# Making three of four one-hot matrices on ScalarE, and other distances in the perceptrons of a graph network

## The chip, the cores and the metric

The kernel runs on one core of a Trainium2 chip. A core has five engines that work side by side and wait for each other through semaphores: TensorE (PE in the profile; its weight loads are PEld), VectorE (DVE), ScalarE (ACT), GpSimd (POOL) and SyncE (SP). The metric is the device time of one execution in microseconds, as the median of three runs. Beside the runs there is one profiled execution, whose trace tells when each instruction ran and what it waited for.

## The reference

The input is 16 graphs (batches) of 1024 nodes with 64 features, and an adjacency of 16 x 1024 x 1024. Four layers follow each other, each with a residual and a layer norm. The first two are matrix products with the adjacency (with a perceptron in the first, with a division by the row sums in the second). The last two are what most of the kernel's time goes into:

```python
nd = adj_d > 0                       # the thinned-out neighbours, and the node itself
vals = jnp.where(nd[..., None], x[:, None, :, :], jnp.inf)
s = jnp.sort(vals, axis=2)           # per node and feature, over the neighbours
...                                  # quantiles 0.25, 0.5, 0.75, interpolated,
...                                  # summed with weights 0.25, 0.5, 0.25 into agg
out = (1.0 + EPS_GIN) * x + agg
h = jax.nn.relu(out @ W1 + b1)
y = h @ W2 + b2
```

So each node sorts its neighbours' features, 64 columns apart from each other, takes three quantiles, and passes the result through a perceptron of two matrix products. Which neighbours count is found once for a graph and serves both layers.

## The kernel before, in words

The nodes of a graph are put in order of the number of their neighbours and cut into eight tiles of 128 nodes. A tile t has room for `SIZES[t]` neighbours: 10, 11, 13, 14, 15, 17, 19 and 33. For each tile the features of the neighbours stand in slots, and a sorting network of minima and maxima runs over the slots on DVE.

The work goes in 18 rounds (`sort_round`). Round k sorts for two members: batch k in the first quantile layer and batch k - 2 in the second. So rounds 2 to 15 have two members, rounds 0, 1, 16 and 17 one. Within a round the seven shorter tiles come first and the long tile, of 33 slots, last.

The slots of the shorter tiles are filled by gathers: POOL issues an indirect DMA for each slot (`gather`, line 362), 92 for a member, from a table in DRAM. A ring of 60 slots (`ROOM`) lets the gathers run some tiles ahead. The slots of the long tile are filled without a gather, by `fill(k)`: for slot i a one-hot matrix `hot` says which node stands in slot i of each row (it is 1 where `e.place` equals i), and `pick` (line 358) multiplies it on PE with the features, split into three bf16 parts, 24 matmuls for each slot. Each group of four slots is copied from PSUM by ACT (line 742, `empty`), and two PSUM areas (`pgs`) take turns. There are six buffers for one-hot matrices (`HOTS`). A matrix is made on DVE by one comparison, or on ACT by two activations: `far` is the distance |place - i| (line 750), and Relu(1 - far) is the matrix (line 752). Before the change ACT makes the matrix of every fourth slot (i % 4 == 3), asked for two slots ahead, and DVE the others, each just ahead of its picks.

After a sort, `weigh` multiplies the wanted slots with the quantile weights on ACT (line 781) and adds them on DVE; `finish` is the perceptron with its layer norm (`settle`). In `finish` the two halves of the nodes go through two matmuls (lines 809 and 816), with an activation between, and a DVE addition `y = pd + b2r` ends each half. Its result for the first quantile layer, x3, is scattered by POOL into a table (line 826), from which the gathers of two rounds later read; `read_back` loads it for the picks of the long tile. For the second layer the same scatter writes the output.

The order of instructions on DVE, ACT and PE is fixed when the program is built, by a planner (`Weave`). All work other than the sorting is a set of Python generators. A `yield n` says that the next piece is due n us of DVE time later, where the DVE time is the sum of the estimated durations of the DVE instructions issued so far (`Metered`; its helper's line 207 stands for nearly all of DVE's instructions in the profile). After each instruction of the sort, `catch_up` issues all pieces that are due. `weave.add(gen, lag, pace)` enters a generator; the pace multiplies all of its distances. `weave.finish` forces a generator to its end, jumping over the distances left. Each engine takes its instructions in the order in which they were issued.

Other generators in the weave: `features` (the first two layers of the next batches), `lists` and `ordered` (the thinned neighbours, the order of nodes, the lists for the gathers). They use ACT for signs with a running sum (lines 526, 570, 585), distances (541) and copies of codes (618), whose results DVE takes up.

Of the kernel before, what the change touches and what calls it, by code (L numbers as in the profile page):

```python
# [13 lines left out]
F16 = mybir.dt.float16  # L14
BF = mybir.dt.bfloat16
I32 = mybir.dt.int32
U8 = mybir.dt.uint8
AF = mybir.ActivationFunctionType
ALU = mybir.AluOpType
AX = mybir.AxisListType  # L20

P = 128
# [7 lines left out]
HOTS = 6  # L30
# [68 lines left out]
def cut_pair(t, view, shift=0):  # L99

    s, m, stride, o, length = view
    s += shift
    if m == 1:
        return t[:, :, s + o : s + o + length, :]
    return t[:, :, s : s + m * stride, :].rearrange("p e (m s) w -> p e m s w", m=m)[:, :, :, o : o + length, :]
# [107 lines left out]
def adj_resnorm_kernel(ctx: ExitStack, tc: tile.TileContext, x, adj_t, nodemask, w01, b01, w02, b02,  # L213
                       w21, b21, w22, b22, w31, b31, w32, b32, out):
    nc = tc.nc
    B, N, C = x.shape
    NT = N // P
# [3 lines left out]
    s = SimpleNamespace()  # L221
    dve = Metered(nc.vector)
# [30 lines left out]
    minus_k = const.tile([P, KW], F32, name="minus_k")  # L253
    nc.gpsimd.iota(minus_k, pattern=[[-1, KW]], base=0, channel_multiplier=0, allow_small_or_imprecise_dtypes=True)
    one_f = const.tile([P, 1], F32, name="one_f")
# [50 lines left out]
    for t, want in enumerate(wants):  # L306
        for first, m, stride, length in regular_runs(want):
            for r in range(m):
                k = first + r * stride
# [44 lines left out]
    def pick(dst, hot, parts, first=True):  # L354

        for c in range(NT):
            for q in range(3):
                nc.tensor.matmul(dst, hot[:, c, :], parts[:, c, q, :], start=first and c + q == 0,  # L358
                                 stop=c == NT - 1 and q == 2)
# [364 lines left out]
    def members(k):  # L724

        return [(m, b, entries[b]) for m, b in enumerate((k, k - 2)) if 0 <= b < B]

    def fill(k):

        while k and (k - 1, NT - 1) not in free:  # L730
            yield 1
        t = NT - 1
        size = SIZES[t]
        got = tails[k] = s.lists.tile([P, 2, size, C], F32, name="got", tag="got_l", bufs=1)
        for m, b, e in members(k):
            while e.parts[m] is None or e.xs[m] is None or e.place is None or e.none is None:
                yield 1
            nc.scalar.copy(got[:, m, 0, :], e.xs[m][:, t, :])
            waiting = None

            def empty():
                nc.scalar.copy(got[:, m, waiting[0] : waiting[0] + 4, :], waiting[1])  # L742

            for i in range(1, size):
                if i % 4 == 1:
                    first, pg = i, pgs[i // 4 % 2]
                if i % 4 == 1:

                    far = s.work.tile([P, NT, P], F16, name="far", bufs=1)
                    nc.scalar.activation(far, e.place, AF.Abs, bias=minus_k[:, i + 2 : i + 3])  # L750
                    by_act = s.lists.tile([P, NT, P], BF, name="hot", bufs=HOTS)
                    nc.scalar.activation(by_act, far, AF.Relu, bias=one_f, scale=-1.0)  # L752
                if i % 4 == 3:
                    hot = by_act
                else:
                    hot = s.lists.tile([P, NT, P], BF, name="hot", bufs=HOTS)
                    dve.tensor_scalar(hot, e.place, float(i), None, op0=ALU.is_equal)
                whole = i < LEAST[t]
                if not whole:
                    nc.tensor.matmul(pg[:, i - first, :], e.none,  # L760
                                     ident_b[: KW - 1, i - 1 : i].to_broadcast([KW - 1, C]), start=True, stop=False)
                pick(pg[:, i - first, :], hot, e.parts[m], whole)
                yield 2.4
                if i % 4 == 2 and waiting:
                    empty()
                if i % 4 == 0:
                    waiting = first, pg
            yield 5
            empty()
            yield 0.5  # L770
            e.filled[m] = True
# [21 lines left out]
    def finish(b, e, layer, agg):  # L793

        xc = e.xs[layer]
        w1s, b1c, w2s, b2r = mlps[layer]
        y = s.work.tile([P, NT, C], F32, name="y_m", bufs=1)
        dve.tensor_add(agg, agg, xc)
        yield 2
        for h in range(NH):  # L800
            pt = s.psum.tile([P, HALF], F32, name="pt", tag="m", bufs=1)
            for q in range(G):
                nc.tensor.transpose(pt[:C, q * P : (q + 1) * P], agg[:, h * G + q, :], ident)
            yield 7
            o_t = s.work.tile([C, HALF], F32, name="o_t", bufs=1)
            nc.scalar.copy(o_t, pt[:C])
            yield 3
            ph = s.psum.tile([P, HALF], F32, name="ph", tag="m", bufs=1)
            nc.tensor.matmul(ph[:H], w1s, o_t, start=True, stop=True)  # L809
            yield 7  # L810
            h_t = s.work.tile([H, HALF], F32, name="h_t", tag="o_t", bufs=1)
            nc.scalar.activation(h_t, ph[:H], AF.Relu, bias=b1c)
            yield 3
            pd = s.psum.tile([P, G, C], F32, name="pd", tag="m", bufs=1)
            for q in range(G):
                nc.tensor.matmul(pd[:, q, :], h_t[:, q * P : (q + 1) * P], w2s, start=True, stop=True)  # L816
            yield 9
            dve.tensor_add(y[:, h * G : (h + 1) * G], pd, b2r[:, None, :].to_broadcast([P, G, C]))
        dve.tensor_mul(y, y, e.mask[:, :, None].to_broadcast([P, NT, C]))
        dve.tensor_add(y, y, xc)  # L820
        xn = agg if layer else s.feat.tile([P, NT, C], F32, name="x3s", bufs=3)
        yield from settle(xn, y, "m")
        yield 1
        dst, rows = (out_rows_of, e.out_rows) if layer else (table[1][b % 3], e.rows)
        for t in range(NT):
            put = nc.gpsimd.indirect_dma_start(  # L826
                out=dst, out_offset=bass.IndirectOffsetOnAxis(ap=rows[:, t : t + 1], axis=0), in_=xn[:, t, :],
                in_offset=None)
            tc.declare_no_dep(put.ins, group=f"rows{layer}{b}", reason="they write different rows")
            tc.add_to_no_dep_group(f"rows{layer}{b}", put.ins)  # L830
        if layer == 0:
            e.xs[1] = xn
            weave.add(read_back(b, e, dst))

    def read_back(b, e, src):

        while b and not entries[b - 1].filled[1]:
            yield 2
        x3 = s.feat.tile([P, NT, C], F32, name="x3", bufs=1)
        nc.sync.dma_start(x3, src[:N, :].rearrange("(t p) c -> p t c", p=P))  # L840
        yield 60
        parts = s.feat.tile([P, NT, 3, C], BF, name="x3p", bufs=1)
        yield from split(x3, parts, x3)
        e.parts[1] = parts
# [42 lines left out]
    weave = Weave()  # L887
# [42 lines left out]
    def finish_round(k, agg, sums):  # L930
        for gen in sums:
            while weave.runs(gen):
                yield 1
        for m, b, e in members(k):
            yield from finish(b, e, m, agg[:, m])

    def sort_round(k):

        if k >= 2:
            weave.finish(rounds[k - 2])  # L940
        filling = weave.add(fill(k), 4.0, 0.7 if k < 3 else 1.0)
        first = members(k)[0][0]
        which = slice(first, first + len(members(k)))
        agg = s.feat.tile([P, 2, NT, C], F32, name="agg")
        sums = []
        for t in (*reversed(range(NT - 1)), NT - 1):
            if t == NT - 1:
                weave.finish(filling)
                got = tails[k]
            else:  # L950
                n = order_of_tiles.index((k, t))
                fetch(n)
                got = gots[n]
            other = s.lists.tile([P, 2, SIZES[t], C], F32, name="other", bufs=1)
            pair = got[:, which], other[:, which]
            for is_max, d, v, i, j, to in usual[t]:
                dve.tensor_tensor(cut_pair(pair[to], v, d if is_max else 0), cut_pair(pair[i], v),
                                  cut_pair(pair[j], v, d), op=ALU.max if is_max else ALU.min)
                weave.catch_up()
                fetch()  # L960
            if len(sums) >= 2:
                weave.finish(sums[-2])
            sums.append(weave.add(weigh(k, t, got, agg, which)))
            weave.catch_up()
        if k:
            weave.finish(rounds[k - 1])
        rounds.append(weave.add(finish_round(k, agg, sums)))

    with ExitStack() as main:
        s.feat = main.enter_context(tc.tile_pool(name="feat", bufs=2))  # L970
# [7 lines left out]
        rounds = []  # L978
# [222 lines left out]
    with tc.If(nc.values_load(over_d[:, B:]) > 0):  # L1201
        with tc.For_i(0, B) as b:
            with tc.If(nc.values_load(over_d[:, ds(b, 1)]) > 0), ExitStack() as general:
# [6 lines left out]
                agg = s.feat.tile([P, NT, C], F32, name="agg")  # L1210
# [65 lines left out]
```

## Time and profile before

| what | value |
|---|---|
| median of 3 runs | 7136.09 us (7135.44 to 7166.32) |
| the profiled execution | 5180.5 us |
| its span, first to last instruction | 5178.8 us |
| mean granted PE clock | 0.756 |
| busy: PE / DVE / ACT / POOL | 3420.0 / 4472.1 / 2755.6 / 3632.1 us |
| one-hot matrices on DVE | 768 of 452 ns |
| one-hot matrices on ACT | 256 of 1150 + 1148 ns |
| gathers | 2944, 1128 ns busy each |

A busy time is the time in which an engine had at least one instruction at work; what it says of the whole span is an average over stages. Waits are given as who waited for whom. The profiled execution is shorter than the runs by 1956 us, and the trace holds nothing of that difference.

### The profile page before, as it was taken

The numbers are of one execution on the slowest core, as the hardware profiler recorded it, in microseconds if no ns is written. First come the engines' busy times: TensorE is split into PE (matmuls) and PEld (weight loads), VectorE is DVE, ScalarE is ACT, GpSimd is POOL, SyncE is SP. The second block draws the span as 40 slices with busy tenths as digits, with TensorE's granted clock in tenths as the row PEclk, the third lists the DMA queues.
The fourth block names the chain that finished last, engine by engine and source line by source line (L and its number), as shares of the span: only waits on it lengthen the run. The fifth ranks groups of instructions, "written<-read, shape, count | busy, mean of one in ns | idle before, by whom it ended". The sixth has DMA issues, their size and how long they took to land. (4 is left out here: it accounts for less than half of the span.)

```text
span 5178.8 us, 109085 instructions
## 1 busy us (share of the span) xinstructions
PE 3420.0 (66%) x43512; PEld 2622.0 (51%) x43512; DVE 4472.1 (86%) x8771; ACT 2755.6 (53%) x6304; POOL 3632.1 (70%) x3229
## 2 busy tenths in 40 slices
PE   6878777486775848687685858677584857343432
PEld 5656656264564726465563636466463645233321
DVE  2488788889899898989989898989989899977976
ACT  3465474565556565565557555565656546233332
POOL 0336574777778787777777787777778787877572
PEclk7887878697877968787787878787796877555555
DMA  3222222122221312222221222222121111111010
GB/s 86 74 54 64 65 57 54 38 59 61 56 62 40 73 42 48 59 57 63 51 65 41 59 46 53 61 56 62 43 73 42 43 45 25 23 24 25 16 26 10
DMA packets 420598, 259.24 MB, mean 50 GB/s; under 512 B 106590, under 2 KB 368878, under 8 KB 420078
## 3 DMA queue, kind: packets, MB, share of 16 engines
q0 software_dynamic: 102400, 105.06, 10.5%
q1 hardware_dynamic: 317678, 147.12, 10.2%
q8 instruction: 342, 5.60, 0.5%
q14 instruction: 178, 1.46, 0.1%
HBM read 239.37 MB, written 12.58 MB: 49 GB/s over the span
## 5 line engine op out<-in xcount | busy, mean ns | idle before, releaser
L362 POOL DMA_INDIRECT got_s<-table,idx x2944 | 3320.8, 1128 | 1358.9 <-issue 675.0
L358 PEld LDWEIGHTS <-hot 128*128 128x128 bf16 x24576 | 961.9, 109 | 843.4 <-DVE hot L207 661.0
L358 PE MATMUL pgk<-x3p,hot 128*128 128x64 bf16 x12288 | 554.2, 213 | 363.1 <-DVE hot L207 328.0
L358 PE MATMUL pgk<-x2p,hot 128*128 128x64 bf16 x12288 | 512.6, 206 | 324.6 <-DVE hot L207 286.3
L520 PE MATMUL pr<-steps,near 128*128 128x512 bf16 x1536 | 421.6, 440 | 288.4 <-ACT junk L526 183.1
L207 DVE TENSOR_TENSOR other<-got_s 128x512 f32<-128x512 f32 (+8 forms) x900 | 512.4, 583 | 102.9 <-DMA got_s<-table,idx 79.6
L781 ACT ACTIVATE got_s<-got_s,wts 128x64 f32<-128x64 f32 x1568 | 399.6, 336 | 236.6 <-DVE got_s L207 235.2
L207 DVE TENSOR_TENSOR got_s<-got_s 128x384 f32<-128x384 f32 (+6 forms) x918 | 491.8, 538 | 19.7
L607 PE MATMUL pk<-near,order 128*128 128x512 f16 x2048 | 473.2, 386 | 0.0
L742 ACT COPY got<-pgk 128x256 f32<-128x256 f32 x256 | 94.5, 369 | 695.0 <-PE pgk L358 686.2
L564 PE MATMUL pv<-minus_n,takes 128*128 128x128 bf16 x1024 | 243.5, 262 | 300.5 <-DVE takes L207 299.9
L520 PEld LDWEIGHTS <-near 128*128 128x128 f16 x1536 | 166.8, 110 | 533.3 <-issue 406.9
L207 DVE TENSOR_TENSOR got_s<-other 128x512 f32<-128x512 f32 (+8 forms) x774 | 407.1, 539 | 7.8
L465 PE MATMUL pa<-x,adj_r 128*128 128x65 f32 x2048 | 348.7, 343 | 64.6 <-ACT x L388 24.6
L207 DVE TENSOR_SCALAR hot<-place 128x1024 bf16<-128x1024 f16 x768 | 343.7, 452 | 37.4 <-PE pgk L358 37.0
L564 PEld LDWEIGHTS <-takes 128*128 128x128 bf16 x1024 | 119.6, 117 | 501.5 <-DVE takes L207 331.1
L465 PEld LDWEIGHTS pa<-x,adj_r 128*128 128x128 f32 x2048 | 335.3, 257 | 67.4 <-ACT x L388 25.3
L563 PE MATMUL pv<-scaled,near 128*128 128x128 f16 x1024 | 244.9, 263 | 166.4 <-ACT near L568 165.2
L207 DVE TENSOR_TENSOR other<-other 128x128 f32<-128x128 f32 (+13 forms) x558 | 320.5, 574 | 15.9
L607 PEld LDWEIGHTS <-order 128*128 128x128 bf16 x2048 | 196.5, 100 | 227.9 <-issue 18.0
L526 ACT ACTIVATE junk<-pr,nb_st 128x1024 f16<-128x1024 f32 x256 | 282.0, 1108 | 51.5 <-PE pr L520 51.2
L752 ACT ACTIVATE hot<-far,one_f 128x1024 bf16<-128x1024 f16 x256 | 294.0, 1148 | 8.4
(202 smaller groups left out, 7196.9 us busy)
## 6 DMA issues: line engine op xcount, KB each, us to landing
adj_r<-in_adj_dram SPq DMA_DIRECT2D x256, 512.0 KB
got_s<-table,idx POOLq DMA_INDIRECT x2944
x_s<-in_x_dram SPq DMA_DIRECT2D x16, 256.0 KB
table<-x SPq DMA_DIRECT2D x16, 256.0 KB
x<-table SPq DMA_DIRECT2D x16, 256.0 KB
table<-x3s,rows POOLq DMA_INDIRECT x128
out_dram<-agg,out_rows POOLq DMA_INDIRECT x128
table<-no_row SPq DMA_DIRECT2D x6, 0.2 KB
```

The source lines that it names most:

```text
L207: return call(*args, **kwargs)
L358: nc.tensor.matmul(dst, hot[:, c, :], parts[:, c, q, :], start=first and c + q == 0, stop=c == NT - 1 and q == 2)
L362: nc.gpsimd.indirect_dma_start(out=dst, out_offset=None, in_=tab, in_offset=bass.IndirectOffsetOnAxis(ap=rows, axis=0))
L465: nc.tensor.matmul(pa[:, q, :], adj[i][:, jt, :], x1[:, jt, :], start=jt == 0, stop=jt == NT - 1)
L520: nc.tensor.matmul(pr[:, h * HALF : (h + 1) * HALF], near[:, c, t * P : (t + 1) * P], steps[:, ONSET + h * HALF - c * P :][:, :HALF], star ...
L526: nc.scalar.activation(junk, prs[t - 1], AF.Sign, bias=lim[:, i, t - 1 : t], scale=-1.0, accum_out=cut_at[:, i, t - 1 : t])
L563: nc.tensor.matmul(pv[:, cols], near[:, c, rows], scaled[:, c, :], start=True, stop=False)
L564: nc.tensor.matmul(pv[:, cols], takes[:, c, rows], minus_n, start=False, stop=False)
L607: nc.tensor.matmul(cols, order[:, c, t * P : (t + 1) * P], left(c, slice(h * G, (h + 1) * G)), start=c == 0, stop=c == NT - 1)
L742: nc.scalar.copy(got[:, m, waiting[0] : waiting[0] + 4, :], waiting[1])
L752: nc.scalar.activation(by_act, far, AF.Relu, bias=one_f, scale=-1.0)
L781: nc.scalar.activation(prods[:, m, i, :], got[:, m, slot_id, :], AF.Copy, scale=e.wts[:, t, i : i + 1])
```

## The change

It has three parts. In `fill`, a matrix is now made on ACT unless i % 4 == 2, so 24 of 32 come from ACT and 8 from DVE. Those of ACT are asked for up to two slots ahead. In `finish`, the distance between the second matmul and the DVE addition goes from 9 to 13. And the finish of rounds 15, 16 and 17 is entered with pace 0.7 in place of 1.0.

```diff
+    def by_act(i):
+        return i % 4 != 2
+
     def fill(k):
...
+            hots = {}
+
+            def make(i):
+
+                hots[i] = s.lists.tile([P, NT, P], BF, name="hot", bufs=HOTS)
+                if by_act(i):
+                    far = s.work.tile([P, NT, P], F16, name="far", bufs=1)
+                    nc.scalar.activation(far, e.place, AF.Abs, bias=minus_k[:, i : i + 1])
+                    nc.scalar.activation(hots[i], far, AF.Relu, bias=one_f, scale=-1.0)
+                else:
+                    dve.tensor_scalar(hots[i], e.place, float(i), None, op0=ALU.is_equal)
+
             for i in range(1, size):
                 if i % 4 == 1:
                     first, pg = i, pgs[i // 4 % 2]
-                if i % 4 == 1:
-
-                    far = s.work.tile([P, NT, P], F16, name="far", bufs=1)
-                    nc.scalar.activation(far, e.place, AF.Abs, bias=minus_k[:, i + 2 : i + 3])
-                    by_act = s.lists.tile([P, NT, P], BF, name="hot", bufs=HOTS)
-                    nc.scalar.activation(by_act, far, AF.Relu, bias=one_f, scale=-1.0)
-                if i % 4 == 3:
-                    hot = by_act
-                else:
-                    hot = s.lists.tile([P, NT, P], BF, name="hot", bufs=HOTS)
-                    dve.tensor_scalar(hot, e.place, float(i), None, op0=ALU.is_equal)
+                for ahead in range(i + 1, min(i + 3, size)):
+                    if by_act(ahead) and ahead not in hots:
+                        make(ahead)
+                if i not in hots:
+                    make(i)
+                hot = hots[i]
...
-            yield 9
+            yield 13
             dve.tensor_add(y[:, h * G : (h + 1) * G], pd, b2r[:, None, :].to_broadcast([P, G, C]))
...
-        rounds.append(weave.add(finish_round(k, agg, sums)))
+        rounds.append(weave.add(finish_round(k, agg, sums), 0.0, 0.7 if k >= B - 1 else 1.0))
```

## The prediction

> **What bounds the kernel now.** I read the page first (busy time, slices, costliest groups), then the stages of one steady round with the busy time of each engine, then the waits of that round and its order of instructions, and last the end of the span.
>
> ```profile
> PE 3420.0 (66%) x43512; PEld 2622.0 (51%) x43512; DVE 4472.1 (86%) x8771; ACT 2755.6 (53%) x6304; POOL 3632.1 (70%) x3229
> DVE  2488788889899898989989898989989899977976
> ACT  3465474565556565565557555565656546233332
> ```
>
> VectorE (DVE) is busy nine tenths in nearly every slice between the start and the last tenth; ScalarE (ACT) about half. A steady round lasts 296 us (the fill of round 6 starts at 1936 us, that of round 7 at 2231 us). I cut it where the fill of the long tile ends:
>
> ```profile
> 1936.00:2101.00 165.00, 144.81 (x2180) 116.56 (x2181) 148.46 (x299) 94.31 (x199) 127.62 (x119) 0.85 0.25 59
> 2101.00:2231.00 130.00, 69.21 (x544) 46.88 (x541) 124.80 (x208) 77.22 (x194) 104.60 (x84) 0.68 0.22 50
> 1936.00:1966.00 30.00, 24.63 (x379) 21.76 (x380) 29.24 (x67) 25.82 (x47) 23.23 (x23) 0.73 0.21 44
> 1996.00:2016.00 20.00, 20.00 (x320) 14.46 (x319) 8.17 (x13) 6.24 (x8) 15.13 (x17) 1.00 0.33 77
> ```
>
> The columns after the length are PE, its weight loads, DVE, ACT, POOL, then clock, DMA share and GB/s. DVE has 273.3 of 295 us; 11.8 of its 21.7 idle us lie in the one stretch 1996 to 2016, where TensorE (PE) is busy all the time. That is one wait:
>
> ```profile
> 2012.24 0.42 DVE L207 TENSOR_TENSOR y_m<-pd,b22r 128x256 f32<-128x256 f32 x1 [11.17 <-PE pd L816]
> ```
>
> So DVE bounds a steady round, with one stall for a late PE. The two kinds of work that trade places:
>
> ```profile
> L207 DVE TENSOR_SCALAR hot<-place 128x1024 bf16<-128x1024 f16 x768 | 343.7, 452 | 37.4 <-PE pgk L358 37.0
> L750 ACT ACTIVATE far<-place,minus_k 128x1024 f16<-128x1024 f16 x256 | 294.5, 1150 | 2.9 <-DVE place L207 2.4
> L752 ACT ACTIVATE hot<-far,one_f 128x1024 bf16<-128x1024 f16 x256 | 294.0, 1148 | 8.4
> ```
>
> The end is bound otherwise. In 4560 to 4760 us DVE waits for gathers, which POOL issues without a break from 4431 to 4711 us:
>
> ```profile
> DVE other L207 <- DMA got_s<-table,idx: 66.0, 5, 18.7
> 4640.00:4680.00 40.00, 11.09 (x174) 9.73 (x174) 21.61 (x42) 12.46 (x36) 30.85 (x31) 0.50 0.13 26
> ```
>
> **What the Trainium skill says.** "ScalarE: Activation LUTs", section "What ACT_TABLE_LOAD costs", prices an activation with a per-partition bias at 280 ns plus 0.833 ns per element, 1133 ns for 1024, and lets neighbours overlap by 93 ns. The trace agrees: 1150 and 1148 ns, and 2.24 us from one pair to the next. "VectorE: DVE Perf Modes", section "The perf-mode tier table", gives this 16-bit tensor-scalar its fastest mode; 452 ns against 2.24 us is a factor of five. "Perfetto Trace Analysis", section "Optimizing Scalar/DVE Operations", says that work may still go to ScalarE when DVE is saturated, which it is here. "TensorE: Matmul & The Clock Gate", table at its head, has DVE and ACT take instructions strictly in order, so a late ACT delays all that is queued behind; the 11.17 us stall, with independent sorting behind it, agrees for DVE.
>
> **The change part by part.** *One-hot matrices.* A fill of one member makes 32, so far 24 on DVE and 8 on ACT, then 8 and 24. There are 32 fills: 512 instructions leave DVE, 512 x 0.452 = 231 us; ACT gets 512 x 2.24 = 1147 us. In a steady round (two members) that is 32 x 0.452 = 14.5 us less DVE on the path that sets the round, and 32 x 2.24 = 72 us more ACT. All of it falls into the 165 us of the fill: ACT there goes from 94.3 to 166 us. The fill is paced by the weave at 2.4 us of DVE time per matrix, and the sum over its stretches decides how late ACT gets. Other ACT work is the busy time less that of the existing pairs (8.97 us in the first 30 us); new pairs are counted from the code, three per four steps and one extra at the start:
>
> - 1936 to 1966: other 16.9, ten pairs 22.4, in 30 us: 9.3 us late
> - 1966 to 1996: 6.8 + 21.0 in 30: 7.1 late
> - 1996 to 2016: 3.9 + 14.0 in 20: 5.0 late
> - 2016 to 2066: 22.1 + 35.0 in 50: 12.1 late
> - to 2106: 8.4 + 24.5 in 40: 5.0 late, and then no pairs until the next fill.
>
> What is queued behind? ACT's signs for the sort keys, its copies of the codes and the layer norms, for which DVE waits. The yields leave 1.4 + 6 us less 1.3 us of work, some 6 us, before the key sum, and 5.5 less 1.0 us before the code's maximum. Of 12 us lateness about 6 become a DVE stall in a round; a stall lets ACT catch up, so they don't add up over it. Bounds 0 (sorting hides it) and 12 us (no slack). I take 6.
>
> The matrices are asked for up to two steps ahead, 4.8 us less 2.24 us for the pair, so PE starts its picks some 9.3 - 2.6 = 6.7 us late at 1966, ahead of the stretch in which it is full anyway. Part of this the DVE stall at the keys has already paid. With six buffers DVE's own matrix i waits for pick i - 3, 7.2 us earlier, a wait that was 37 us in the whole span; it isn't the tighter limit.
>
> *Longer distance in the perceptrons (9 to 13).* The stalled addition is that of the second half. It moves 8 us of DVE work later, but its matmuls move 4 us later too, behind 4 us more of PE's queue. At most 4 us of the stall go; if the late PE is then met by the code's maximum (PE slack about 7 us), none. PE's later start takes some back: +7 to -4, and I take -1.5 us. Each x3 is scattered about 8 us later: that of batch 5 ended at 2052 and the gathers that read it began at 2067, so this lies in the ring's lead; without it POOL would wait up to 8 us.
>
> A steady round: -14.5 + 6 - 1.5 = -10 us. Eleven such rounds (3 to 13): **-110 us**. Here POOL is no limit: 184 gathers and 16 scatters at 1.25 us are 250 us, below 286.
>
> *Rounds 0 to 2.* DVE saves 29 us, but these fills run at pace 0.7, 1.7 us a step, against 1.7 us of ACT pairs a step: ACT is full before anything else. Bounds -20 and +20, taken as 0.
>
> *The end.* Round 14 saves about 10 us up to the point at which the gathers of round 15 run without a break; round 15 nothing but some 3 us after its last gather; round 16 5 us. *Pace 0.7 in the last finishes:* after the tail sort of round 15 (ends 4814) the weighing (22 us of yields) and the finish (87 us) put x3 of the last batch at 4925 to 4936; the last 92 gathers start at 4939 and end at 5077, with DVE waiting for them. The finish becomes 95 x 0.7 = 66 us, so this chain starts 20 us sooner. Bounds 0 and -28; I take -20. What could give it back is the gathers of round 16, which end at 4896: 10 us after that they may start. Sum of the end: **-38 us**. The later finishes are at the mercy of nothing but latency.
>
> In all -148 us: the profiled execution of 5180.5 us (span 5178.8, 1.7 around it) should become 5032. The median of the runs is 7136.09, 1956 us more, and no view shows where those are. I take them as a constant, so 7136 - 148 = **6988 us**; if the runs were the profile stretched by 1.38, it would be 6932.
>
> **The rivals.**
> *ACT late at no cost.* Sorting doesn't depend on ACT, which speaks for it; against it stand the short yields. 11 x (-14.5 - 4) - 45 = -249: 6887 us.
> *A wash.* ACT becomes the bound of the fill: the 12 us become stalls in full, and PE's lateness costs 2. Then rounds 3 to 13 give nothing, and the end 38, of which half may be lost to the gathers: 7117 us.
> *Slower: PE starved at the head of the fill.* Each us that late matrices cost PE before 1966 is a us more in the block 1966 to 2016, where PE is full, and on DVE behind it. Now PE waits for DVE's matrices there for 7.1 us at once; with ACT saturated it could wait at each pick. It decides once stalls grow by 14.5 + 38/11 = 18 us a round. At 25 us: 11 x 10.5 - 38 = +77, 7213 us. Against it: the two steps ahead.
> *It doesn't do what it says* I can exclude for the count of DVE matrices (768 to 256); for the pace in the end, the gathers may set the time anyhow, which is +20 in the forecast.
>
> **How the numbers follow.** Forecast 0.54 (own range 6925 to 7060), no cost 0.17, wash 0.16, slower 0.13. 0.5% is 36 us, about what a measurement of this kernel can tell from no change: faster means below 7100, which takes the first two and a fifth of the wash, 0.74; same 0.13; slower 0.13. The range runs from 6870, below the no-cost case, to 7130, above the wash, and leaves out the slower case and some stretched ones.
>
> **What would show it.** DVE matrices x256 and pairs x768 on ACT; DVE busy near 4240 us, ACT near 3900; a steady round of 286 us, with ACT nearly full in its first 165; new DVE waits for ACT (codes, key sums) of a few us per round; the wait for pd shorter than 11 us or replaced by the code's maximum; x3 of the last batch 20 us sooner after the tail sort of round 15. I am wrong if rounds stay at 296 us with PE waiting for ACT's matrices, if POOL waits for x3 in each round, or if the unseen 1956 us hide another bound.

## The result, and the profile after

The change made the kernel slower: 7442.93 us (median of 4 runs, 7429.76 to 7447.9) against 7137.33 us, a ratio of 1.0415 with a 95% interval of 1.0386 to 1.0445. The forecast was 6988 us and faster.

One thing has to be told first. In the runs of this study the unchanged kernel took either about 5170 us (on three chips) or about 7130 us (on two others, and in the runs of the result), and all kernels that ran together on one chip were of one kind; I take it as a property of the chip. So the profiled execution of the kernel before, 5180 us, most likely comes from another chip than its runs of 7136 us. All ratios below compare kernels on one chip. I call the two the quick and the slow chip; the result above is from a slow one. A second profile of the unchanged kernel, taken on a slow chip later, stands beside the changed one here.

From the page of the kernel before, on a slow chip (span 7102.0 us), the busy time of each engine with its share:

```profile
PE 3928.4 (55%) x43478; PEld 2893.2 (41%) x43512; DVE 4483.5 (63%) x8771; ACT 2756.5 (39%) x6304; POOL 3472.5 (49%) x3229
```

From the page of the changed kernel, on a slow chip (span 7446.2 us):

```profile
PE 4005.7 (54%) x43475; PEld 2939.3 (39%) x43512; DVE 4307.0 (58%) x8259; ACT 3883.1 (52%) x7332; POOL 3434.7 (46%) x3229
L207 DVE TENSOR_SCALAR hot<-place 128x1024 bf16<-128x1024 f16 x256 | 110.1, 430 | 1552.5 <-PE pgk L358 999.3
L754 ACT ACTIVATE far<-place,minus_k 128x1024 f16<-128x1024 f16 x768 | 879.3, 1145 | 9.4 <-DVE place L207 2.4
L755 ACT ACTIVATE hot<-far,one_f 128x1024 bf16<-128x1024 f16 x768 | 881.8, 1148 | 45.6 <-remote 20.5
```

The change did to the counts what it says: 256 matrices on DVE, 768 on ACT, each at about its old duration. DVE was busy 177 us less and ACT 1127 us more. But on a slow chip DVE is busy only 63% of the time before the change, so its work alone doesn't set the round there. What stands beside it is seen in the waits of PE. The first three lines are from the kernel before on a slow chip, as who waited for whom, us in total, times, longest:

```profile
PE pgk L358 <- issue: 967.8, 1140, 13.7
PE pgk L358 <- ACT got L742: 224.0, 75, 28.5
PE pgk L358 <- DVE hot L207: 187.4, 27, 96.4
```

The waits of PE in the changed kernel on a slow chip:

```profile
PE pgk L358 <- issue: 876.5, 1006, 18.8
PE pgk L358 <- ACT hot L755: 378.2, 28, 95.0
PE pgk L358 <- ACT got L745: 288.6, 62, 31.3
PE pgk L770 <- ACT got L745: 236.7, 74, 13.0
```

"issue" is idle time in which PE waited for nothing that the profile shows. On a slow chip it comes to 1.6 ms over all of PE's instructions, in both kernels (1633 and 1601 us); on a quick chip to 12 and 17 us. What the change added to PE's waits on the slow chip are those for ACT: for its matrices and for its copies out of PSUM.

The same two kernels on a quick chip show the effect of the change without that. A steady round of the kernel before there, cut where the fill of the long tile ends (after the length: PE, weight loads, DVE, ACT, POOL, clock, DMA share, GB/s):

```profile
1934.00:2110.00 176.00, 154.91 (x2279) 124.62 (x2279) 158.70 (x320) 95.97 (x205) 133.44 (x126) 0.84 0.27 61
2110.00:2230.00 120.00, 54.86 (x448) 37.14 (x448) 115.32 (x187) 76.12 (x190) 95.34 (x76) 0.71 0.21 45
```

The same round of the changed kernel on a quick chip:

```profile
2068.00:2273.00 205.00, 159.59 (x2372) 130.28 (x2372) 153.42 (x297) 177.00 (x293) 151.44 (x145) 0.81 0.22 54
2273.00:2393.00 120.00, 53.24 (x352) 31.96 (x350) 109.70 (x177) 66.20 (x171) 77.54 (x56) 0.69 0.16 42
```

DVE does 10.9 us less in the round, and the round is 29 us longer (20 on average over the eleven steady rounds, 3 to 13). All of it is in the fill, where ACT is now busy 177 of 205 us. DVE's waits in this round before the change, on a quick chip:

```profile
DVE y_m L207 <- PE pd L816: 11.4, 1, 11.4
DVE deg L207 <- PE pa L465: 1.3, 1, 1.3
DVE best L207 <- ACT code L618: 0.9, 1, 0.9
```

and after it:

```profile
DVE counted L207 <- PE pn L692: 10.1, 2, 7.8
DVE hot L207 <- PE pgk L358: 8.1, 2, 7.9
DVE key_c L207 <- ACT junk L585: 8.0, 1, 8.0
DVE rows L207 <- ACT sorted_own L642: 6.4, 1, 6.4
DVE best L207 <- ACT code L618: 5.8, 2, 3.7
DVE takes L207 <- ACT dist L541: 5.1, 2, 2.8
DVE ln_st_m L207 <- ACT ln_st_m L383: 4.3, 1, 4.3
```

One stall on PE has become many stalls, each in another chain of work. In this round DVE's waits grew from 14 to 54 us, 36 of them on ACT. On average over the eleven rounds they grew from 14.6 to 44.2 us: on ACT from 0.8 to 26.2, on PE from 13.7 to 18.0. DVE's work fell by 10.2 us, and the difference is the 20 us by which a round got longer. On a slow chip the sum is much the same (work 11 us less, waits 29 us more, the round 18 us longer).

### The profile page after: what moved, and what is told of

Read it like the earlier page. It is cut to its first block, busy times and chain, and to the rows that moved or that the text cites. A ratio compares the mean times of both kernels' runs of the same rounds, so it can differ in the third digit from the quotient of the medians.

```text
span 7446.2 us, 109584 instructions
## 1 busy us (share of the span) xinstructions
PE 4005.7 (54%) x43475; PEld 2939.3 (39%) x43512; DVE 4307.0 (58%) x8259; ACT 3883.1 (52%) x7332; POOL 3434.7 (46%) x3229
## 5 line engine op out<-in xcount | busy, mean ns | idle before, releaser
L362 POOL DMA_INDIRECT got_s<-table,idx x2944 | 3116.5, 1059 | 3601.8 <-DVE other L207 941.0
L358 PEld LDWEIGHTS <-hot 128*128 128x128 bf16 x24576 | 1115.0, 114 | 2063.1 <-issue 1611.1
L358 PE MATMUL pgk<-x3p,hot 128*128 128x64 bf16 x12288 | 662.0, 219 | 790.4 <-issue 472.7
L358 PE MATMUL pgk<-x2p,hot 128*128 128x64 bf16 x12288 | 662.0, 215 | 782.7 <-issue 403.8
L207 DVE TENSOR_SCALAR hot<-place 128x1024 bf16<-128x1024 f16 x256 | 110.1, 430 | 1552.5 <-PE pgk L358 999.3
L755 ACT ACTIVATE hot<-far,one_f 128x1024 bf16<-128x1024 f16 x768 | 881.8, 1148 | 45.6 <-remote 20.5
L754 ACT ACTIVATE far<-place,minus_k 128x1024 f16<-128x1024 f16 x768 | 879.3, 1145 | 9.4 <-DVE place L207 2.4
L207 DVE TENSOR_TENSOR got_s<-got_s 128x384 f32<-128x384 f32 (+7 forms) x918 | 490.5, 538 | 48.0 <-ACT got_s L791 13.8
L434 PE MATMUL px<-adj_r,x_s 128*64 128x128 f32 x2048 | 336.0, 326 | 37.5 <-issue 32.4
L434 PEld LDWEIGHTS px<-adj_r,x_s 128*64 128x64 f32 x2048 | 288.5, 168 | 76.6 <-issue 64.9
```

Of the source, the lines that this page charges most:

```text
L207: return call(*args, **kwargs)
L362: nc.gpsimd.indirect_dma_start(out=dst, out_offset=None, in_=tab, in_offset=bass.IndirectOffsetOnAxis(ap=rows, axis=0))
L434: nc.tensor.matmul(px[C:, q * P : (q + 1) * P], x_s[:, jt, :], adj[t][:, jt, :], start=jt == 0, stop=jt == NT - 1)
L755: nc.scalar.activation(hots[i], far, AF.Relu, bias=one_f, scale=-1.0)
```

## The experiments

The theories at the start: A, the added ACT work makes the loss, by lateness; B, the new distances make it; C, the order of the queues makes it (matrices asked for ahead, the six buffers, fewer DVE us to pace the planner); and beside these, where the unseen 1956 us are.

**The kernel before, profiled again.** No edit.

> The kernel before, unchanged, profiled again. The profile shown with it lasted 5180 us and the runs 7136; the profile of the changed kernel lasted 7446, like its runs, and PE stood idle in it for 1577 us with nothing it waited for ('issue'), against 109 us in the 5180 us profile. Theory A (PE is held up in its own issue, and the profile shown was of an execution without that): this profile lasts about 7136 us, with over 1000 us of such PE idle time, DVE busy still 4470 us. Theory B (the 1956 us lie outside the span): span again 5180 us.

(The letters in this expectation are its own, and not those above.) It took 5174.76 us, with 5172.48 as the median of the kernel before on the same chip. That is the picture of neither of its two theories, since here the runs too were quick. So the 1956 us lie neither outside the span nor in an odd execution; they belong to the chip. Later the same kernel met a slow one:

> The kernel before, unchanged. Where it takes some 7130 us, the trace should show PE idle for over 1000 us with nothing that it waits for, as all traces of that chip, and some 100 us of that where it takes 5172; DVE busy the same 4470 us in both.

7103.75 us, DVE busy 4483.5 us, and 1633 us of "issue" on PE, 967.8 of them in the one group of matmuls shown above. So on a slow chip PE is held up in its own issue, as the first of the two theories had it.

**One part alone, twice.** The one-hot part with the old distances, and the distances with the old matrices:

```diff
-            yield 13
+            yield 9
...
-        rounds.append(weave.add(finish_round(k, agg, sums), 0.0, 0.7 if k >= B - 1 else 1.0))
+        rounds.append(weave.add(finish_round(k, agg, sums)))
```

> Only the one-hot part of the change: 24 of 32 matrices on ACT, asked for two ahead; distance 9 and pace 1.0 as before. If the matrices make the loss: 7400 to 7460 us. If the distances do: at or below 7136 us.

> Only the distances: 13 for 9 and pace 0.7 in the last rounds; one matrix of four on ACT as before. If the matrices make the loss: 7080 to 7160 us. If the distances do: near 7440 us.

The matrices alone: 5451.33 us, 1.0534 (1.0510 to 1.0558). The distances alone: 5186.54 us, 1.0028 (1.0018 to 1.0038). The numbers expected were for a slow chip, but the split is plain: the matrices make the loss. The whole change on a quick chip:

> The whole change once more, on a chip where the kernel before may take 5172 us. If the parts add up there: 5451 + 14 = 5465 us, a ratio of 1.057. If the longer distance gives PE and ACT the time they need: below 5451 us.

5471.66 us, 1.0596 (1.0578 to 1.0613), 303 us slower than the kernel before. On the slow chip it is 306 us. The parts add up to 293 us.

**Less of it: two of four on ACT.**

```diff
-        return i % 4 != 2
+        return i % 2 == 1
```

> As the one-hot part alone, but two of four matrices on ACT (odd i). ACT full in the fill as the cause: ACT has 130 of 165 us there in place of 166, so most of the loss goes, near 7150 us. Matrices asked for ahead (order of the queues) as the cause: the loss stays, above 7300 us.

5221.76 us, 1.0099 (1.0076 to 1.0122). Half of the added ACT work is there, and less than a fifth of the loss (49 of 279 us). A steady round took 295 us, as before the change: ACT 129.85 of 174 us in the fill,

```profile
1963.00:2137.00 174.00, 147.88 (x2287) 119.52 (x2288) 151.68 (x301) 129.85 (x241) 135.05 (x125) 0.86 0.26 61
```

and the 6 us that DVE saved went into waits. Most of the loss lay in the first rounds: round 5 began 31 us later than in the kernel before. There the fill and the lists go at shortened distances (0.7 and 0.6). The rest of the 41 us by which the two profiled executions differ came after round 13. The test of the first rounds keeps one of four in rounds 0 to 2:

> As e_half (two of four matrices on ACT, 5222 us where the kernel before takes 5172), but one of four in rounds 0 to 2. If the loss of e_half is in the start (round 5 began at 1669 us, against 1638 in the kernel before): 5185 to 5195 us. Else 5215 to 5225.

It met a slow chip: 7126.92 us against 7126.72, 1.0004 (0.9985 to 1.0022). There is no loss, as expected of the start. But the kernel with two of four in all rounds was not run on a slow chip, so how much of its loss these rounds make is not shown by this pair.

**The same queues with less ACT time.** The activations cover half of the columns, and the picks read that half twice, so this kernel's picked features are not the reference's.

```diff
-                    nc.scalar.activation(far, e.place, AF.Abs, ...
-                    nc.scalar.activation(hots[i], far, AF.Relu, ...
+                    nc.scalar.activation(far[:, : NT // 2], e.place[:, : NT // 2], AF.Abs, ...
+                    nc.scalar.activation(hots[i][:, : NT // 2], far[:, : NT // 2], AF.Relu, ...
```

> As the one-hot part alone (5451 us on a chip where the kernel before takes 5172), but the two activations of a matrix cover 512 of its 1024 columns, and the picks read these twice (so the picked features of those slots are not the reference's). Order of all queues, DVE's work and the picks stay; ACT's pair falls from 2.24 to about 1.3 us, its work in the 165 us of a fill from 166 to some 120. ACT's load as the cause: 5050 to 5200 us. The order of the queues (matrices asked for ahead, six buffers, fewer DVE us to pace the planner) as the cause: above 5400 us.

5150.53 us, 0.9969 (0.9958 to 0.9980). Two lines of its groups on ACT show the size of the edit:

```profile
L755 ACT ACTIVATE hot<-far,one_f 128x512 bf16<-128x512 f16 x768 | 554.4, 722 | 24.9
L754 ACT ACTIVATE far<-place,minus_k 128x512 f16<-128x512 f16 x768 | 552.0, 719 | 9.5 <-DVE place L207 2.4
```

The two kinds together are 655 us shorter, with the same instructions in the same queues, and 301 us come back. In the steady rounds DVE's waits on ACT fell from 23.3 us with the matrices alone to 8.5. That is the main test: the cause is ACT's time, as in theory A, and not the order, as in C. It also bounds the gain: even so ACT has 137 of 176 us in the fill of round 7, and of the work taken from DVE only 0.3% of the time is left as profit.

**Is PE held up by the copies out of PSUM?** With the matrices alone, PE waited 567 us for ACT's copies of the groups of four slots. DVE makes these copies here:

```diff
-                nc.scalar.copy(got[:, m, waiting[0] : waiting[0] + 4, :], waiting[1])
+                dve.tensor_copy(got[:, m, waiting[0] : waiting[0] + 4, :], waiting[1])
```

> As the one-hot part alone, but DVE and not ACT copies the groups of four slots out of PSUM (256 copies of some 0.4 us, 6 to 7 us more DVE work in a round). If a late ACT holds PE up through the two PSUM areas (567 us of PE waits for these copies, against 115 in the kernel before): these waits go, 5250 to 5380 us. If PE is held up by late matrices, or DVE by ACT directly: 5450 to 5550 us.

5445.89 us, 1.0538 (1.0521 to 1.0556): nothing. DVE now waits for the picks, as ACT did,

```profile
DVE got L207 <- PE pgk L358: 564.9, 149, 15.9
```

and PE waits for ACT's matrices, 461 us in all (409 with the matrices alone). So the copies only passed the lateness on. The run is no clean test of the PSUM areas, since DVE now stands in its own order of instructions where ACT stood before.

**The same work at a lower rate.** The fill at 2.9 us of DVE time for a matrix:

```diff
-                yield 2.4
+                yield 2.9
```

> As the one-hot part alone (5451 us), but the fill goes at 2.9 us of DVE time a matrix in place of 2.4, so the same ACT work is spread over some 190 us in place of 165. If the rate asked of ACT makes the loss: 5200 to 5350 us. If it is the amount of ACT work in a round, or the order of the queues: 5430 to 5480 us.

5445.01 us, 1.0525 (1.0507 to 1.0542). A miss for the idea that the rate in the fill alone is the cause. ACT was busy 178 of 217 us in the fill of round 6, so it had some room, and the loss stayed. The waits had moved: fewer for the keys (87 us in place of 126), new ones at the end (94 in place of 34), where the sort of the long tile stood ready before its slots were. So the lower rate brought a cost of its own, and the amount of ACT work in a round stays as possible a cause as its rate in the fill. From the waits of this kernel:

```profile
DVE other L207 <- ACT got L745: 94.0, 15, 13.6
DVE key_c L207 <- ACT junk L585: 87.4, 15, 10.9
```

**Longer distances for all that waits for ACT.** Distances of the first layers, lists and perceptrons times 1.2, the fill as it was:

```diff
-            pace = 0.6 if b < 4 else 1.0
+            pace = 0.6 if b < 4 else 1.2
...
-        rounds.append(weave.add(finish_round(k, agg, sums)))
+        rounds.append(weave.add(finish_round(k, agg, sums), 0.0, 1.2 if 3 <= k < B - 1 else 1.0))
```

> As the one-hot part alone (5451 us), with all distances of the first layers, the lists and the perceptrons 1.2 times as long from batch 4 and round 3 on; the fill keeps its own. Latency as the cause: the DVE waits of a steady round fall from 45 towards 20 us, 5200 to 5300 us. Throughput of ACT as the cause: 5420 to 5480 us.

7771.36 us on a slow chip, 1.0912 (1.0875 to 1.0949): worse than all others, and no answer to its question. In the part of round 8 after the fill, DVE was busy 112.65 of 207 us, and waited 60.8 us in one piece for a code:

```profile
3939.00:4146.00 207.00, 102.03 (x762) 62.97 (x762) 112.65 (x156) 62.45 (x136) 63.45 (x65) 0.65 0.13 31
DVE best L207 <- ACT code L618: 60.8, 1, 60.8
```

I read it so that the chain that makes a batch's lists no longer fits into a round, and the sorting that would cover it runs out. Whether moderate distances would give back the loss stays open.

**Where the gain of the longer distance in the perceptrons goes.** With the distances alone the stall of 11.4 us on the perceptron is gone, but rounds last 286 and 304 us by turns. The waits of a long one (the round from 2227 us):

```profile
DVE near L207 <- DMA adj_r<-in_adj_dram: 12.0, 1, 12.0
DVE hot L207 <- PE pgk L358: 8.9, 1, 8.9
```

In the long rounds the read-back of x3 leaves SP's queue 149 us into the round, after the scatter that it waits for; the first of eight adjacency loads follows 0.4 us behind it, the last within some 36 us. In the short rounds the read-back leaves at 127 us and the first load at 133. Two tries to take it out of the way, 20 and 55 us later:

```diff
+        yield 55
         x3 = s.feat.tile([P, NT, C], F32, name="x3", bufs=1)
         nc.sync.dma_start(x3, src[:N, :].rearrange("(t p) c -> p t c", p=P))
-        yield 60
+        yield 8
```

> The distances alone (5187 us), with the read-back of x3 put on SP's queue 20 us of DVE time later, and the wait after it 40 in place of 60. With the distances alone every other round lasted 304 us in place of 286, with some 12 us in which DVE waits for the adjacency. If the adjacency loads stand behind the read-back in SP's queue, which waits for a scatter that is now later: all rounds 286 us, 5060 to 5110 us. If it is something else (DMA bandwidth, the buffers of the loads): 5170 to 5200 us.

> The distances alone (5187 us where the kernel before takes 5172), with the read-back of x3 put on SP's queue 55 us of DVE time later, and 8 in place of 60 after it. 20 us later did nothing: in the slow rounds the read-back still left at 149 us of the round, when the scatter had landed, and the adjacency loads behind it at 149 to 151 us in one go. At 55 us it comes after the loads of its round. If the queue is the cause: no more waits of 12 us for the adjacency, all rounds near 286 us, 5040 to 5110 us. If it is the rate of the loads: 5170 to 5200 us.

5183.49 us, 1.0034 (1.0019 to 1.0048), and 5224.42 us, 1.0106 (1.0085 to 1.0126). Neither answers the question, as neither edit did what was meant. With 20 us the long rounds stayed. With 55 us all rounds last about 300 us, with 9.3 us of waits for the adjacency on average, and the read-back still stands ahead of the loads: in rounds 5 to 8 it leaves at 143 to 145 us and the first load 0.4 us later, so that every round now looks like the long ones. That fits the queue as the cause, but no run took the read-back out of the way, and it is not shown. The pace of the last rounds, taken out of the second one:

> As e_late, with pace 1.0 in the last rounds as before. If the quicker finish shortens the end by the predicted 20 us: 20 us above e_late. If it takes in rounds 14 to 16 what it gives in round 17 (in the run of the distances alone: 22 us longer rounds there, 20 us shorter last one): within 8 us of e_late.

5237.8 us, 1.0122 (1.0101 to 1.0143), 13 us more, with intervals that overlap. In the traces the last scatter of x3 ends 109 us after the tail sort of round 15 with pace 0.7, and 132 us after it without: 23 us, of which some 13 reach the end. That is the pace by itself. Against the kernel before, the longer distance takes part of it back: the same time was 122 us before, 112 with the distances alone and 115 with the whole change, on quick chips.

**ACT work where ACT is idle.** Two of four matrices on ACT only for the second member of a round, one of four for the first, first with the late read-back, then without it and from round 3 on:

```diff
+    def by_act(k, m, i):
+        return i % 4 == 3 or (k >= 3 and m == 1 and i % 4 == 1)
```

> As e_late, with two of four matrices on ACT for the second member of a round and one of four for the first. DVE saves 8 x 0.45 = 3.6 us in a round of two members, ACT gets 18 us where it is least busy. If ACT has room there: 30 to 50 us below e_late. If any more ACT work in the fill comes back as waits: the same or above.

> The kernel before with pace 0.7 in the last rounds, and two of four matrices on ACT for the second member from round 3 on. The pace alone is worth some 13 us, the matrices 11 x 3.6 us of DVE work: 5120 to 5150 us if ACT has room there, 5160 to 5175 if not.

> As e_mix, with the distance of 13 in the perceptrons. If this distance costs by itself, as in the run of the distances alone (+0.3% with the pace, so about +27 us without it): 25 us above e_mix. If less DVE work by the side changes where it stands: the same or below.

> e_mix once more. Where the kernel before takes 7130 us: 0.8% faster, as before. Where it takes 5172 us: 5120 to 5150 us.

With the late read-back: 5154.87 us, 0.9965 (0.9953 to 0.9976), 70 us below the same kernel with one of four; DVE was busy 49 us less, and the rest is not explained. From round 3 on, on slow chips: 7064.65 us, 0.9922 (0.9894 to 0.9950), and again 7056.9 us, 0.9919 (0.9890 to 0.9948). With the distance of 13 added: 7088.4 us, 0.9943 (0.9924 to 0.9962), 24 us more, near the 25 expected, though the intervals overlap. So the version without it, which includes the pace of 0.7, beats both kernels, by 0.8% over the one before on a slow chip; on a quick one it was not run. The gain is not that of the pace: in the two traces from one slow chip rounds 3 to 13, which the pace doesn't touch, went from 4626 to 4533 us, and the rest from 1088 to 1115. Whether it is the smaller dose or its place in the second member was not separated. In a round of two members it makes 24 of 64 matrices on ACT; the change studied makes 48, the kernel before 16.

## Why the prediction was wrong

The sum by stretches, cut at the first picks of rounds 3 and 14 in the traces. On a quick chip: rounds 0 to 2 went from 1039 to 1109 us, rounds 3 to 13 from 3257 to 3475, the rest from 877 to 882. On a slow chip: 1388 to 1470, 4626 to 4829, 1088 to 1147. The prediction had 0, -110 and -38.

- **DVE's saving** (14.5 us in a steady round): the matrices left DVE as counted, and its busy time in the round shown fell by 10.9 us, 10.2 on average. Mis-sized by a quarter to a third. The price of 0.452 us was the duration of an instruction; the whole span on a quick chip has DVE 164 us less busy for 512 matrices, 0.32 us each. In the trace of before, on a quick chip, a matrix starts before the instruction ahead of it ends (1942.60 + 1.22 = 1943.82), and ends after the next one starts:

```profile
1942.60 1.22 DVE L207 TENSOR_TENSOR other<-got_s 128x1024 f32<-128x1024 f32 x1
1943.74 0.42 DVE L207 TENSOR_SCALAR hot<-place 128x1024 bf16<-128x1024 f16 x1
1944.08 1.22 DVE L207 TENSOR_TENSOR got_s<-got_s 128x1024 f32<-128x1024 f32 x1
```

- **How late ACT gets** (9.3 us after the first 30, 12.1 at most): right. For batches 4 to 13 on quick chips the eight signs of the keys ended 15.9 us after their matmuls before the change and 25.8 us with the matrices alone, 9.9 us later. (The later stretches of the working count some 52 pairs where a round makes 48, so the 12.1 was a little high.)
- **What of that becomes a stall** (6 us, bounds 0 and 12): this step failed. DVE's waits in a steady round grew by 29.6 us on average, in place of 6, or of 12 at most. One part is the slack before the key sum, put at 6 us. In the trace of before the key sum follows 4.6 us after the last sign. With the matrices alone the signs end 9.9 us later, and DVE, with less of its own to do, is ready 3.1 us sooner; so it waits 8.6 us there (9.9 + 3.1 - 4.6 is 8.4), and it never waited there before in these rounds. The larger part is "they don't add up over it": the key sum is only one of ten kinds of wait in the round shown, and those on ACT together grew by 25.4 us a round on average. A stall didn't let ACT catch up: it had been asked for 166 us of work in the 165 us of the fill, and was busy 177 us of 205. From the code I take it that a fill that is paced by DVE's time asks ACT for the next matrices as soon as DVE moves on.
- **Longer distance** (-1.5 us): the distances alone gave rounds of 286 and 304 us by turns and nothing on average (3264 us for the eleven rounds, against 3257). The stall on the perceptron did go, from 10.7 us a round to 0.1. What took its place was what is late next, as the prediction feared, but that was the adjacency and the buffers of the matrices, not the code's maximum.
- **Rounds 0 to 2** (0, bounds of 20): +70 and +82 us. The reason given, ACT full before anything else, fits the trace (in the fill of round 1 ACT was busy 107 of 113 us, before the change 69 of 83), and should have made this a loss in the forecast. With two of four matrices on ACT, too, most of the loss came in these rounds.
- **The end** (-38): x3 of the last batch came 7 to 10 us sooner after the sort in place of 20, as the 23 us of the pace are partly eaten by the longer distance, and with the distances alone the time from round 14 on was 878 us against 877. The shorter rounds 14 and 16 did not come. (That POOL issues gathers without a break from 4431 to 4711 us was misread: it pauses from 4582 to 4593.)
- **The unseen 1956 us as a constant**: the difference between the kernels is the same on both kinds of chip, 303 and 306 us, so the number held. That was luck, since the premise behind it did not hold. On a slow chip DVE has 275 us of work in a round of 421, and what grew is PE's time: of the 1929 us between the two traces of the kernel before, PE was busy for 529 more and idle at "issue" for 1621 more, and its waits for others shrank by 228. So the profile shown was no profile of the chip of the runs. A view that misses a quarter of the time can't say what bounds the rest.
- **The rivals**: what came has the sign of the slower one and the mechanism of the wash, ACT as the bound of the fill, at more than twice its size: of the 29.6 us more waits in a round 25.4 are on ACT directly and 4.3 on PE. The slower case was given 0.13, and its loss of 77 us is a quarter of the measured one. Its turning point of 18 us more stalls in a round was too high, as it used the saving of 14.5 us: with two of four matrices 5.4 us more waits already ate all of the 5.7 us saved.

Shown: that the matrices make the loss, and that ACT's time in them, not their order, does. Argued only: that it is the lateness in each single chain. For the keys it is measured, but the lower rate, which eased the keys, gave nothing back, so the amount of ACT work in a round is not excluded as the cause.

## What to carry to other kernels

Before work goes to an engine that is half idle, add up its load in the stretch where the work lands, and take the slack of what waits for it from the trace (how long the steps really took, with what stands between them), not from the planner's distances: at 166 us asked for in 165 no slack is left, and an engine in the middle of many chains can pass its lateness on in each of them. Here spreading the work over a longer fill gave nothing back, and less time of ACT for each matrix gave back all. Small doses can still pay: 8 more matrices in a round, in the second member only, gave 0.8% (with the pace of the last rounds), 16 more left the steady rounds as they were, 32 more cost 4 to 6%. And price the work that leaves an engine by the busy time that goes with it, not by the duration of its instructions. And where the profiled time and the runs differ by a quarter, find out why before arguing from the profile.

## What the runs showed of the hardware

The same program took 5172 us on some chips and 7127 us on others, steadily on each. On the slow ones PE often stands idle between instructions with nothing to wait for that the profile shows, as here for 0.5 to 1.9 us at a time, in the middle of a group of matmuls on one and the same matrix. From the order of instructions on PE in the changed kernel on a slow chip:

```profile
2636.69 0.98 PE L358 MATMUL pgk<-x3p,hot 128*128 128x64 bf16 x15
2638.28 0.22 PE L358 MATMUL pgk<-x3p,hot 128*128 128x64 bf16 x1 [0.61 <-issue]
2640.38 0.21 PE L358 MATMUL pgk<-x3p,hot 128*128 128x64 bf16 x1 [1.88 <-issue]
2641.12 0.23 PE L358 MATMUL pgk<-x3p,hot 128*128 128x64 bf16 x1 [0.53 <-issue]
```

Fifteen matmuls pass in 0.98 us, and the next ones come one by one. The matmuls themselves are little longer: in the kernel before those of the picks from x3 take 213 ns on a quick chip and 219 on a slow one. The mean granted PE clock is lower on the slow one, 0.682 against 0.759; whether as a cause or as a consequence of the idle time is open. DVE and ACT show no slower instructions: in the changed kernel DVE's matrix takes 430 ns on a slow chip and 437 on a quick one, ACT's second activation 1148 ns on both. What holds PE's issue up was not settled.

On DVE an instruction's duration is more than what it costs: neighbours overlap, and a matrix of 452 ns took 0.32 us of DVE's busy time with it when it left. On ACT, where the two activations of a matrix last 1145 and 1148 ns, 512 more matrices brought 1127 us of busy time, 2.20 us each; with half of the columns the two last 719 and 722 ns.
